# Taking the maximum of attention logits by image column first, and adding the column bias to 32 maxima

## The chip, the cores and the metric

The kernel runs on one NeuronCore of a Trainium2 chip, in float32 throughout. The metric is the device time of one execution in microseconds (us); lower is better. A second, profiled execution gives the trace. The engines are named as in the profile: PE (TensorE's matmuls), PEld (its weight loads), DVE (VectorE), ACT (ScalarE), POOL (GpSimd) and SP (the queue that issues the DMAs).

## The reference

Eight images of 32 x 32 pixels with 256 channels go through two layers: a hybrid of convolution and attention, and then attention with a mixture of experts. The change is in the attention of the first layer, which has 8 heads of 8 channels and a logit with three terms:

```
logits  = einsum('bnid,bnjd->bnij', q, k)     # i: query pixel, j: key pixel, 1024 each
logits += rel_w                               # depends on the query and on the key's column
logits += rel_h                               # depends on the query and on the key's row
weights = softmax(logits, axis=-1)
attn    = einsum('bnij,bnjd->bnid', weights, v)
```

The softmax needs the maximum of each query's logits over 1024 keys. In the kernel's names a key is a pair (x, y): x is the image row, y the column (0 to 31 each). So a logit is s(x, y) + w(y), where s holds the product and the row term and w is the column term.

## The kernel before, in words

Images are handled one after the other in a loop over `b`. For each, `conv_layer_inputs` normalizes the image, computes keys, queries and values, and builds the relative terms: `rh` holds the row terms, `rwq` (128 queries x 8 tiles x 2 head groups x 128) the column terms with queries on partitions, as `(y h)` with h one of four heads. `conv_layer_attention` does the attention and, beside it, the 3 x 3 convolution (L398, its results added by VectorE in L406). `attention_layer` does the second layer's attention; the experts come at the end, for all images.

Inside `conv_layer_attention` the work is cut into four `Unit`s of an image: two groups of four heads (`HG = 4`) times two halves of the queries. A unit loads its tile `F` by DMAs on SP's queue (L423, L427, L434: row terms, queries, column terms), and then passes through three sweeps:

- `score` (16 per unit, two per step): for 128 queries and one head, two products (L448) of 24 rows of `F` with 512 columns of `km` each fill `lg`, a PSUM tile of 2 x 512. There are two such tiles. VectorE then reads the tile in L457: it adds the column term, spread over the 32 image rows, and keeps the maximum, which goes to one column of `mx`. A second instruction of L457 reads out the accumulated maximum.
- `fold` (L465 to L474, once per unit): the 16 columns of maxima are negated, transposed, added to the row terms and written into `F` by DMA, so that the next sweep gets logits less their maximum.
- `weigh` (32 per unit, four per step): the product (L483) for 128 keys and 512 queries into a PSUM tile `st` (three of them), and ScalarE's exponential (L490) from there to `PT`. `gather` (L498) multiplies `PT` of a finished key tile with the values, four products per step that use all 128 rows of the array. At the end of a unit come `close` and `settle` (L508 to L518).

A product of 24 or 32 rows occupies one of four groups of 32 rows of the array; products on different groups run side by side. `r = 32 * ((hl + 2 * a) % HG)` says which group.

PE's order is written out by hand in a loop over steps `s` (`tc.manual_schedule`). Step `s` issues `score(2j)`, `weigh(k, 1)`, `weigh(k, 3)`, `score(2j + 1)`, `weigh(k, 0)`, `gather` of the step before, `weigh(k, 2)`. Weighing starts 10 steps after scoring (`lead = NT + LAG`). In these first 10 steps there is nothing to weigh, and the image's 144 convolution products are spread over them (`if not weigh and left`). Steps 10 to 31 score and weigh; steps 32 to 41 only weigh. The order of the other engines is set by the framework from the program's order and the tiles' dependences.

`km` holds the keys' side of both products, in the order `p e (x y)`: 4 blocks `e` of 8 columns, and in each 16 image rows x by 8 columns y. `weigh` takes a block of 128 as it lies. `score` reads it through a view, `p x e y`, so that the 512 columns of `lg` come in the order of image rows, each with its 32 columns.

Of the kernel before, what the change touches and what calls it, by code (L numbers as in the profile page):

```python
# [9 lines left out]
FP = mybir.dt.float32  # L10
I32 = mybir.dt.int32
AF = mybir.ActivationFunctionType
ALU = mybir.AluOpType
AX = mybir.AxisListType
PSUM = bass.MemoryType.PSUM

P = 128
B, HH, WW, C = 8, 32, 32, 256
# [4 lines left out]
HG = 4  # L23
# [12 lines left out]
def kernel(  # L36
# [26 lines left out]
    nc = tc.nc  # L63
# [29 lines left out]
    with ExitStack() as ph:  # L93
        wp = ph.enter_context(tc.tile_pool(name="wp", bufs=1))
        work = ph.enter_context(tc.tile_pool(name="work", bufs=1))
# [15 lines left out]
        def lg_tile(name):  # L111
            return ps_lg.tile([P, 2, 512], FP, tag="lg", name=name)
# [80 lines left out]
        KM = []  # L193
# [215 lines left out]
        class Unit:  # L409
# [32 lines left out]
            def score(self, n, rwq):  # L442

                i, hl = divmod(n, HG)
                lg = lg_tile("lg")
                for a in range(2):
                    r = 32 * ((hl + 2 * a) % HG)
                    nc.tensor.matmul(  # L448
                        lg[:, a, :],
                        lhsT=self.F[r : r + 24, a, 0, i * P : (i + 1) * P],  # L450
                        rhs=KM[self.g][r : r + 24, a].rearrange("p e (x y) -> p x e y", y=8),
                        start=True,
                        stop=True,
                    )
                lv = lg.rearrange("p a (x y) -> p (a x) y", y=WW)
                bias = rwq[:, self.half * 4 + i, self.g, hl::HG].unsqueeze(1).to_broadcast([P, HH, WW])
                nc.vector.tensor_tensor_reduce(  # L457
                    lv, lv, bias, 1.0, -3.0e38, op0=ALU.add, op1=ALU.max, accum_out=self.mx[:, i, hl : hl + 1]
                )

            def fold(self, n):

                mc = mcols[n % 2]
                for c in (0, 64):
                    nc.vector.tensor_scalar(mc[:, :, c : c + HG], self.mx, -1.0, None, ALU.mult)  # L465
                pm = st_tile("pmx")
                for i in range(4):
                    nc.tensor.transpose(pm[0:68, i * P : (i + 1) * P], mc[:, i, :], ident)
                mb = work.tile([P, 512], FP, tag="mb", name="mb")
                nc.vector.tensor_tensor(mb[0:68], pm[0:68], self.rh[0:68], ALU.add)  # L470
                F = self.F
                for a, r, c in ((0, slice(0, P, 32), slice(0, 4)), (1, slice(64, P, 32), slice(64, 66)), (1, slice(0, 64, 32), slice(66, 68))):
                    k = c.stop - c.start
                    nc.sync.dma_start(out=F[r, a], in_=mb[c].unsqueeze(1).to_broadcast([k, 4, 512]))  # L474
# [55 lines left out]
        def conv_layer_attention(b, kq, rh, rwd, rwq):  # L530
# [7 lines left out]
            for s in range(NU * NT + lead + 2):  # L538
# [3 lines left out]
                if j == 0 and 0 < u < NU - 1:  # L542
                    units.append(Unit(u + 1, kq, rh, rwd))
                score, weigh = u < NU, 0 <= w < NU
                if score:
                    units[u].score(2 * j, rwq)
# [212 lines left out]
    work = ctx.enter_context(tc.tile_pool(name="fwork", bufs=2))  # L759
# [148 lines left out]
    for b in range(B):  # L908
# [22 lines left out]
        for q in range(2):  # L931
            hT = work.tile([P, TOPK * NF, 512], FP, tag="hT", name="hT")
            for k in range(TOPK):
                for f in range(NF):
                    phd = ps_h.tile([P, 512], FP, tag="h", name="phd")
                    for kc in range(KC):
# [3 lines left out]
                            rhs=n2T[:, kc, q * 512 : (q + 1) * 512],  # L940
# [6 lines left out]
            r = work.tile([P, 4, C], FP, tag="r", name="r")  # L947
            st = work.tile([P, 4, 6], FP, tag="fst", name="fst")
            mv = work.tile([P, 4, 2], FP, tag="fmv", name="fmv")
            for j in range(4):  # L950
                py = ps_y.tile([P, C], FP, tag="y", name="py")
                nc.tensor.matmul(py, lhsT=dbc[:, b, :], rhs=b2sb, start=True, stop=False)  # L952
                for k in range(TOPK):
                    for f in range(NF):
# [3 lines left out]
                            rhs=ws[k][1][:, f, :],  # L958
# [6 lines left out]
            y = work.tile([P, 4, C], FP, tag="yo", name="yo")  # L965
# [58 lines left out]
```

## Time and profile before

| | us |
|---|---|
| median of 3 runs | 3249.84 (3228.76 to 3250.91) |
| profiled execution | 3222.47, its span 3220.7 |
| PE busy | 2910.0 (90% of the span) |
| VectorE busy | 1707.5 (53%) |
| ScalarE busy | 966.6 (30%) |
| GpSimd busy | 291.6 (9%) |
| L448 (scores), 2048 matmuls | 599.7 |
| L457 (maxima), 512 tiles | 1011.7, and 87.8 for reading the accumulator |
| L483 (weigh), 2048 matmuls | 695.6 |
| L490 (exponentials), 1024 | 568.1 |

The span is the time from the first to the last instruction of the profiled execution; the device time lies 1.8 us above it. The profiled execution is 27 us below the median of the three runs. Busy time counts an instruction from its start to its end; the ends of matmuls are modelled, and a busy PE can be waiting within. An fp32 product shows up as two matmul instructions (passes). Rows of groups give the busy time in us, the mean time of one instruction in ns, then the idle time of the engine before them and what ended it. The granted clock of PE (PEclk) is a share of full speed: in this trace it is 1.00 or 0.50, with a mean of 0.911.

### The profile page before, as it was taken

To read this page: it belongs to the slowest core of one execution; us is meant where nothing else is said; L and a number is where in the kernel's file an instruction comes from. 1 tells how busy PE (TensorE), PEld (TensorE's weight loads), DVE (VectorE), ACT (ScalarE), POOL (GpSimd) and SP (SyncE) were. 2 spreads that over 40 slices of the span, in tenths; PEclk is the share of its full clock that TensorE was granted. 3 is DMA by queue.
4 is the path that set the end of the run, shared out by engine and by line. 5 is a ranking of instruction groups with operands and counts; after the bars stand their busy time and mean duration, and the time that the engine had idled before them with its cause. 6 is when DMAs were issued, how large, how long until landed. Compare 5 with 4: busy or idle time off the path is not lost.

```text
span 3220.7 us, 40512 instructions
## 1 busy us (share of the span) xinstructions
PE 2910.0 (90%) x16473; PEld 1691.7 (53%) x16473; DVE 1707.5 (53%) x2734; ACT 966.6 (30%) x1657; POOL 291.6 (9%) x321
## 2 busy tenths in 40 slices
PE   5998899889988998899889998899889986999999
PEld 4633673367335832584257425753565344666665
DVE  4792469245934594448444844486448734233322
ACT  1153105420542054204520352035302531323222
POOL 4001100110011000100011001100110012112110
PEclk7999789979998899889987998799979997999999
DMA  3310131014100510051004100410032102112110
GB/s 101 57 29 1 56 67 29 1 42 81 29 2 29 93 29 2 27 92 32 2 27 93 30 4 14 92 36 12 1 78 37 25 1 95 66 63 81 53 59 20
DMA packets 83753, 135.75 MB, mean 42 GB/s; under 512 B 12000, under 2 KB 40552, under 8 KB 81520
## 3 DMA queue, kind: packets, MB, share of 16 engines
q1 hardware_dynamic: 80976, 131.20, 18.0%
q8 instruction: 130, 2.13, 0.3%
q10 hardware_dynamic: 2592, 1.97, 0.2%
q14 instruction: 55, 0.45, 0.1%
HBM read 53.43 MB, written 25.17 MB: 24 GB/s over the span
## 4 chain that ended last, share of the span: by engine, by line
PE 80%; DVE 8%; issue 6%; ACT 3%; SPq 1%; DMA 1%; POOL 1%; ACTq 0%; DVEq 0%; POOLq 0%
PE pc L398 13%; PE st L483 11%; PE lg L448 10%; PE py L955 7%; PE phd L937 7%; PE po L498 7%; PE lg L593 4%; PE po L705 3%; PE prel L338 3%; PE pq L673 2%; PE tp L610 2%; PE pk L294 2%; PE pmean L736 2%; PE py L952 1%; DVE lg L457 1%
## 5 line engine op out<-in xcount | busy, mean ns | idle before, releaser
L457 DVE CUSTOM_DVE_ANT_1 lg<-lg,rwq 128x1024 f32<-128x1024 f32 x512 | 1011.7, 2041 | 212.5 <-PE lg L448 194.0
L483 PE MATMUL st<-F,km 32*128 32x512 f32 x2048 | 695.6, 655 | 46.1 <-ACT PT L490 45.5
L490 ACT ACTIVATE PT<-st 128x512 f32<-128x512 f32 x1024 | 568.1, 597 | 556.0 <-PE st L483 526.0
L448 PE MATMUL lg<-km,F 24*128 24x512 f32 x2048 | 599.7, 650 | 22.1 <-DVE mx L457 13.6
L398 PEld LDWEIGHTS pc<-convw,gpad 128*128 128x128 f32 x2304 | 388.5, 197 | 66.7 <-issue 66.7
L398 PE MATMUL pc<-convw,gpad 128*128 128x192 f32 x2304 | 412.1, 339 | 0.0
L483 PEld LDWEIGHTS st<-F,km 32*128 32x128 f32 x2048 | 213.2, 186 | 340.8 <-ACT PT L490 306.7
L448 PEld LDWEIGHTS lg<-km,F 24*128 24x128 f32 x2048 | 198.7, 191 | 207.2 <-DVE mx L457 113.7
L498 PE MATMUL po<-PT,v 128*32 128x512 f32 x2048 | 285.7, 619 | 0.0
L955 PE MATMUL py<-w,hT 128*128 128x256 f32 x1024 | 237.3, 385 | 0.0
L937 PE MATMUL phd<-n2T,w 128*128 128x512 f32 x512 | 224.3, 596 | 0.0
L658 POOL TENSOR_TENSOR T<-T,n 128x256 f32<-128x256 f32 x64 | 47.2, 752 | 1933.5 <-DVE n L653 1933.5
L955 PEld LDWEIGHTS py<-w,hT 128*128 128x128 f32 x1024 | 189.9, 190 | 45.6 <-issue 22.4
L962 DVE TENSOR_TENSOR r<-py,n 128x256 f32<-128x256 f32 x64 | 27.2, 425 | 309.3 <-PE py L955 309.3
L517 DVE RECIPROCAL rc<-pa 128x16 f32<-128x16 f32 x32 | 8.9, 277 | 297.8 <-PE pa L514 297.8
L490 ACT ACT_TABLE_LOAD x8 | 10.3, 1283 | 498.2 <-PE st L483 498.2
L937 PEld LDWEIGHTS phd<-n2T,w 128*128 128x128 f32 x512 | 97.2, 191 | 115.3 <-issue 108.2
L498 PEld LDWEIGHTS po<-PT,v 128*32 128x32 f32 x2048 | 41.7, 109 | 205.0 <-issue 199.4
L593 PE MATMUL lg<-k,q 128*128 128x512 f32 x256 | 129.1, 624 | 0.0
L705 PE MATMUL po<-pt,v 128*128 128x256 f32 x512 | 120.5, 381 | 5.5 <-DVE pt L613 5.5
L596 DVE TENSOR_REDUCE nm<-lg 128x1 f32<-128x1024 f32 x64 | 78.4, 1224 | 80.2 <-PE lg L593 80.2
L944 ACT ACTIVATE hT<-phd,b1c 128x512 f32<-128x512 f32 x128 | 86.3, 686 | 97.0 <-PE phd L937 96.8
(212 smaller groups left out, 2664.5 us busy)
## 6 DMA issues: line engine op xcount, KB each, us to landing
F<-rh SPq DMA_DIRECT2D x256, 128.0 KB
F<-kq SPq DMA_DIRECT2D x256, 64.0 KB
F<-rwd SPq DMA_DIRECT2D x256, 64.0 KB
w<-in_L_ffn_W_dram SPq DMA_DIRECT2D x32, 512.0 KB
T<-in_x_dram SPq DMA_DIRECT2D x8, 1024.0 KB
rwd<-rw SPq DMA_DIRECT2D x16, 512.0 KB
Td<-T SPq DMA_DIRECT2D x8, 1024.0 KB
T<-Td SPq DMA_DIRECT2D x8, 1024.0 KB
```

Source lines behind the costliest of these rows:

```text
L338: nc.tensor.matmul(dst, lhsT=lhsT, rhs=kqv[rows, :, a], start=True, stop=True)
L398: nc.tensor.matmul(pc[:, 0:CO], lhsT=gflat[:, dx, kc, t * P + dy * WW : (t + 1) * P + dy * WW], rhs=convw[:, i, :], start=i == 0, stop=i = ...
L448: nc.tensor.matmul(lg[:, a, :], lhsT=self.F[r : r + 24, a, 0, i * P : (i + 1) * P], rhs=KM[self.g][r : r + 24, a].rearrange("p e (x y) -> ...
L457: nc.vector.tensor_tensor_reduce(lv, lv, bias, 1.0, -3.0e38, op0=ALU.add, op1=ALU.max, accum_out=self.mx[:, i, hl : hl + 1])
L483: nc.tensor.matmul(st, lhsT=KM[self.g][r : r + 32, a, e, :], rhs=self.F[r : r + 32, a, e, :], start=True, stop=True,)
L490: nc.scalar.activation(self.pts[j][:, hl, :], st, AF.Exp)
L498: nc.tensor.matmul(self.po[32 * hl : 32 * hl + 32, :], lhsT=v32[:, j, self.g * HG + hl, :], rhs=pt[:, hl, :], start=j == 0, stop=j == NT - 1,)
L593: nc.tensor.matmul(lg[:, h, :], lhsT=q, rhs=k[:, h * 512 : (h + 1) * 512], start=True, stop=True)
L705: nc.tensor.matmul(po[:, 0:IB], lhsT=v1[:, jc, :], rhs=pt[:, jc, :], start=jc == 0, stop=jc == NT - 1)
L937: nc.tensor.matmul(phd, lhsT=ws[k][0][:, kc, f * P : (f + 1) * P], rhs=n2T[:, kc, q * 512 : (q + 1) * 512], start=kc == 0, stop=kc == KC - 1,)
L944: nc.scalar.activation(hT[:, k * NF + f, :], phd, AF.Gelu, bias=b1c[:, f, k * B + b : k * B + b + 1])
L955: nc.tensor.matmul(py, lhsT=hT[:, k * NF + f, j * P : (j + 1) * P], rhs=ws[k][1][:, f, :], start=False, stop=k == TOPK - 1 and f == NF - 1,)
```

## The change

The logits' maximum is taken in two stages. The maximum over the image rows x comes first, for each column y: a plain reduce of `lg` into 32 numbers, which leaves the column term out, since it is the same for all rows. The 32 numbers of four heads are collected in a new tile `my` (32 columns by 4 heads). After the fourth head the column term is added to all 128 numbers, and a second reduce takes the maximum over the columns for the four heads at once. The products of `score` read `km` through another view, `p e y x` in place of `p x e y`: the 512 columns of `lg` now come by image column, each with its 16 rows, and in `km` one column of the moving operand lies 8 elements (32 bytes) from the one before it. Instruction for instruction, the order of PE stays as it was. The diff shifts later lines by 7.

```diff
             def score(self, n, rwq):
 
                 i, hl = divmod(n, HG)
+                if hl == 0:
+                    self.my = work.tile([P, WW, HG], FP, tag="my", name="my", bufs=2)
+                my = self.my
                 lg = lg_tile("lg")
                 for a in range(2):
                     r = 32 * ((hl + 2 * a) % HG)
                     nc.tensor.matmul(
                         lg[:, a, :],
                         lhsT=self.F[r : r + 24, a, 0, i * P : (i + 1) * P],
-                        rhs=KM[self.g][r : r + 24, a].rearrange("p e (x y) -> p x e y", y=8),
+                        rhs=KM[self.g][r : r + 24, a].rearrange("p e (x y) -> p e y x", y=8),
                         start=True,
                         stop=True,
                     )
-                lv = lg.rearrange("p a (x y) -> p (a x) y", y=WW)
-                bias = rwq[:, self.half * 4 + i, self.g, hl::HG].unsqueeze(1).to_broadcast([P, HH, WW])
-                nc.vector.tensor_tensor_reduce(
-                    lv, lv, bias, 1.0, -3.0e38, op0=ALU.add, op1=ALU.max, accum_out=self.mx[:, i, hl : hl + 1]
-                )
+
+                nc.vector.tensor_reduce(
+                    my[:, :, hl], lg.rearrange("p a (y x) -> p y a x", y=WW), AX.XY, ALU.max
+                )
+                if hl == HG - 1:
+                    nc.vector.tensor_tensor(
+                        my, my, rwq[:, self.half * 4 + i, self.g].rearrange("p (y h) -> p y h", h=HG), ALU.add
+                    )
+                    nc.vector.tensor_reduce(self.mx[:, i, :], my.rearrange("p y h -> p h y"), AX.X, ALU.max)
```

## The prediction

> **What bounds the kernel now.** I read the costliest groups first, then looked at one image (82 to 274 us of the trace) stage by stage, and last at what each engine waits for in the stage in which the change works.
>
> The groups of the page, with some of the longer list that keeps shapes apart:
>
> ```profile
> L457 DVE CUSTOM_DVE_ANT_1 lg<-lg,rwq 128x1024 f32<-128x1024 f32 x512 | 1011.7, 2041 | 212.5 <-PE lg L448 194.0
> L483 PE MATMUL st<-F,km 32*128 32x512 f32 x2048 | 695.6, 655 | 46.1 <-ACT PT L490 45.5
> L490 ACT ACTIVATE PT<-st 128x512 f32<-128x512 f32 x1024 | 568.1, 597 | 556.0 <-PE st L483 526.0
> L448 PE MATMUL lg<-km,F 24*128 24x512 f32 x2048 | 599.7, 650 | 22.1 <-DVE mx L457 13.6
> ...
> L457 DVE DVE_READ_ACCUMULATOR2_ANT mx<- 128x1 f32 x512 | 87.8, 171 | 0.0
> ...
> L596 DVE TENSOR_REDUCE nm<-lg 128x1 f32<-128x1024 f32 x64 | 78.4, 1224 | 80.2 <-PE lg L593 80.2
> ...
> L350 DVE COPY rw<-prel 128x512 f32<-128x512 f32 x32 | 30.2, 1022 | 76.9 <-PE prel L338 76.9
> ```
>
> L457 is the largest group of VectorE: 2.04 us for each of 512 tiles. L596 takes the maximum of a PSUM tile of the same size in 1.22 us, so a plain maximum costs 0.82 us less. L448 has 2048 matmul instructions for 1024 products: an fp32 product runs as two passes.
>
> Next the stages of the first image, cut where the first and the last `weigh` and the last `score` start:
>
> ```profile
> core 0: us, PE busy (x) PEld busy (x) DVE busy (x) ACT busy (x) POOL busy (x), PEclk, DMA share, GB/s
> 82.00:138.00 56.00, 56.00 (x350) 47.13 (x349) 38.32 (x46) 0.00 (x0) 0.00 (x0) 1.00 0.43 79
> 138.00:232.00 94.00, 91.04 (x526) 31.79 (x528) 87.50 (x96) 48.87 (x88) 0.00 (x0) 0.96 0.14 25
> 232.00:274.00 42.00, 37.29 (x184) 10.12 (x178) 4.82 (x9) 23.30 (x43) 0.00 (x0) 1.00 0.01 2
> ```
>
> Three stages, alike in all eight images. **Lead** (10 steps, scores and convolution): PE never idles, VectorE has a third of the time free. **Mixed** (22 steps, scores, exponentials and gathers): VectorE is busy 87.5 of 94 us. **Tail** (no scores): PE and ACT alone. So VectorE can set the pace in the mixed stage only. The waits of its steady part, 150 to 232 us, say that it does, mildly:
>
> ```profile
> PEld st L483 <- ACT PT L490: 16.5, 20, 0.8
> ...
> PEld lg L448 <- DVE mx L457: 13.8, 16, 1.5
> ...
> DVE lg L457 <- PE lg L448: 3.7, 4, 3.1
> ```
>
> VectorE waits 3.7 us for scores, PE waits 13.8 us for VectorE to free a score tile. What stands just behind VectorE is seen in the tail, one step of which is:
>
> ```profile
> 260.81 1.06 PE L498 MATMUL po<-PT,v 128*32 128x512 f32 x8
> ...
> 261.80 1.13 PE L483 MATMUL st<-F,km 32*128 32x512 f32 x6
> 262.96 1.57 ACT L490 ACTIVATE PT<-st 128x512 f32<-128x512 f32 x3 [1.45 <-PE st L483]
> ...
> 263.61 1.12 PE L483 MATMUL st<-F,km 32*128 32x512 f32 x2 [0.67 <-ACT PT L490]
> 264.66 1.06 PE L498 MATMUL po<-PT,v 128*32 128x512 f32 x8
> ```
>
> Gather to gather 3.85 us with no score and no L457: three `st` tiles filled, one exponential, the fourth matmul, the gather. That loop of PE and ACT stays whatever VectorE does. In the mixed stage the gathers of the trace follow each other by 4.11 us (mean of 14 regular steps of each image) and by 4.76 us in the four steps with a `fold` or a `settle`, which cost 4.50 in the tail.
>
> **The change, part by part.**
>
> *VectorE.* Removed: 512 times 2.04 + 0.17 us (L457 and its read of the accumulator, which partly overlaps the next L457). Added: 512 reduces of 128x1024 to 32 columns. By L596 they cost 1.22 us; their reading hops between the two halves of `lg` every 16 columns, which no row shows, so the bounds are 1.22 and L457's own 2.04. I take 1.23, since L596 is the same operation on the same memory and L382, which writes in runs of 8, costs no more than the plain copy L367 (0.69 us for 512 columns both). Added too, per four scores: an add of 128x128 (nearest L518, 0.29 us) and a reduce to 4 columns (nearest L154 below, 0.36 us). Per step of two scores VectorE falls from 4.1 us to 2 x 1.23 + 0.65 / 2 = 2.8 us. The add waits for the fourth reduce and the last reduce for the add, all on VectorE; queued behind them are the next L459 reduce, the convolution's L406, and `fold`'s operations. These come earlier than now, since the queue in front of them is shorter.
>
> In lead and tail none of this is on the path: in the lead L457 and L406 fill 38 of 56 us under a PE that never idles. In the mixed stage the step can fall to the loop: 14 x (4.11 - 3.85) + 4 x (4.76 - 4.50) = 4.6 us per image, 37 for eight; 40 with the two first steps. That is the most the change can bring.
>
> *PE.* No instruction is added or moved: L448 keeps its 2048 passes and `lg` is still written in one run. But the order in which the passes read `km` changes: now runs of 8 columns that lie together, after the change each column is 8 columns (32 bytes) from the one before. Now L448 behaves like a contiguous read: its passes on one row group start 0.43 us apart in the trace, as L593's do. What does a read with a step cost? The trace has one such moving operand, L338 (step of 32 columns), and two strided VectorE operations:
>
> ```profile
> L154 DVE TENSOR_REDUCE esel<-ident x1: 362/362/362, 2.2 to 2.2; 128x32 f32<-128x128 f32 x1
> ...
> L146 DVE TENSOR_REDUCE gsel<-ident x1: 287/287/287, 1.9 to 1.9; 128x16 f32<-128x128 f32 x1
> ...
> 389.36 1.02 DVE L350 COPY rw<-prel 128x512 f32<-128x512 f32 x1 [4.94 <-PE prel L338]
> ```
>
> VectorE pays: L154 reads 128 columns at a step of 128 bytes and takes 75 ns longer than L146, 0.59 ns a column; L350 writes 512 columns at that step in 1022 ns where L367 takes 692, 0.64 ns a column. Contiguous columns cost it (1224 - 692) / 512 = 1.04 ns, so a strided one is about 1.63 to 1.69 ns. PE at half clock (granted 0.50 there) does not pay: from the start of the last weight load of L338 to VectorE's L350 the trace has 505 ns; for L375, same weight load, 64 contiguous columns, to L382 it has 561. The 56 ns between them are 32 columns at 1.67 ns (at half clock the trace has 1095 ns from the last pass of L448, 512 columns, to VectorE and 459 from L923's, 128 columns: 1.66 ns a column). Were strided columns twice as dear, the two would be equal. So memory gives PE a strided column in at most 1.67 ns, and that is all the row says: at full clock PE wants one in 0.43 us / 512 = 0.83 ns. The bounds at full clock are thus 0.43 us a pass (nothing lost) and 512 x 1.67 = 0.85 us. Between them I take 1.64 ns, 0.84 us a pass, by the VectorE rows, which give nearly the time that PE had at half clock: it looks like one limit of the memory, not of an engine.
>
> [...] The row at half clock shows no penalty, the two VectorE rows do. [...]
>
> What 0.41 us a pass cost: in the lead, four products of a step run at once on four row groups, two passes each, and the convolution needs all rows, so the step grows by 2 x 0.41 = 0.83 us. About 9 of the 10 steps run at full clock (the first falls into the half clock of 407 to 413 us in the second image, likewise in the others): 9 x 0.83 x 8 = 59 us, all on PE's path. In the mixed stage the scores run beside `weigh` on other row groups, but one product of each pair shares a row group with the weigh that comes first: 0.96 + 2 x 0.84 + 0.20 us drain = 2.84 us into the step; two reduces end it at 4.07 and 5.30. The next step's first score, due at 3.85, waits for the tile until 4.07, its second one until 5.30 and ends 0.25 us after the gather could start. So the step is 3.85 + 0.25 = 4.10: as now, and the gain is gone. Bounds there: -2 us an image where the waits hide better (-16), and, with a reduce of 1.5 us (a third of the way to its upper bound), ends 0.27 and 0.54 us later, 0.41 a step on the mean, 20 x 0.41 x 8 = 65.
>
> Sum: 0 + 59 + 0, say 60. The profiled execution took 3222.5 us, the median is 3249.8, with runs from 3228.8 to 3250.9; the profile lies 27 us under the median, and I add the 60 to the median: **3310 us**, 1.8% slower. Its own range: 44 us of lead (0.83 + 0.59 = 1.43 ns a column, were VectorE's extra time what counts: 9 x 2 x 0.30 x 8) with -16 in the mixed stage, to 62 with 65, 3278 to 3376.
>
> **The rivals.**
>
> *A: PE reads the step for nothing.* The half-clock row is for it; against it are the VectorE rows. Then only VectorE's relief counts: -24 (a second `score` that still holds the row group of a weigh for 0.1 us a step) to -40, about -36: 3214 us.
>
> *B: the strided reduce is the dear part.* PSUM hops make L459 as dear as L457 was (2.04 us), PE pays nothing. VectorE then needs 4.08 + 0.33 = 4.41 us a step against 4.11: 20 x 0.30 x 8 = 48 us slower, 3298. It decides from a reduce of 1.9 us on. Against it: L596, and that the runs of 16 are longer than those of L382, which cost nothing.
>
> **How the numbers follow.** Forecast 0.67, A 0.25, B 0.08. A measurement of this kernel tells about 1% from no change. A lies on that border: 0.14 of it is faster by over 1%, 0.11 within. The forecast gives 0.05 within 1%, 0.62 slower, B 0.01 and 0.07. Together 0.14, 0.17, 0.69. The range reaches from most of A to the upper end of the forecast: 3206 to 3370.
>
> **What would show it.** Right: L448's successor with passes 0.8 us apart on a row group, the lead stage longer by 7 us an image (62.7 to 67.0 us from first score to first weigh now), the mixed stage about 93.6 us as now, VectorE busy some 390 us less, L459 near 1.23 us. Wrong: passes still 0.43 us apart, the lead unchanged, and mixed-stage gathers 3.85 us apart (A); L459 at 1.9 us or more with VectorE full in the mixed stage (B).

## The result

The changed kernel took 3355.97 us (median of 3 runs, 3351.31 to 3364.85) against 3249.84 us: a ratio of 1.035, with an interval of 1.030 to 1.041. The profiled execution took 3364.85 us, 142 us more than the profiled one before. Single runs of one kernel differ by the clock that PE was granted (in one series of the kernel before, mean clocks of 0.895 to 0.915 went with 3271 to 3217 us), so sums are made stage by stage below.

The groups of the profile page after; L451, L459, L490, L497 and L505 were L448, L457, L483, L490 and L498:

```profile
L459 DVE TENSOR_REDUCE my<-lg 128x32 f32<-128x1024 f32 x512 | 604.1, 1221 | 619.4 <-PE lg L451 599.7
L451 PE MATMUL lg<-km,F 24*128 24x512 f32 x2048 | 746.7, 1108 | 0.4 <-issue 0.4
L497 ACT ACTIVATE PT<-st 128x512 f32<-128x512 f32 x1024 | 558.1, 598 | 641.5 <-PE st L490 330.5
L490 PE MATMUL st<-F,km 32*128 32x512 f32 x2048 | 697.8, 657 | 41.0 <-ACT PT L497 40.5
```

VectorE's reduce costs 1.22 us, as L596 did, and now waits 600 us for scores. The scores' passes went from 650 to 1108 ns while `weigh`, which reads the same `km` as it lies, stayed at 657. One burst of eight score passes in the lead stage, from the timeline of PE, before and then after:

```profile
108.87 1.14 PE L448 MATMUL lg<-km,F 24*128 24x512 f32 x8
```

```profile
105.61 2.09 PE L451 MATMUL lg<-km,F 24*128 24x512 f32 x8
```

Four row groups run two passes each, side by side: the four first passes start within 0.02 us of each other. A burst is longer by 0.95 us. In the trace the second pass of a burst now starts 0.98 us after the first (0.53 before, 0.11 of which is the first weight load), and two passes in the middle of a row of strided ones start 0.90 us apart (0.43 before).

The stages of the first image, cut as before at the first and last `weigh` and the last `score`, with the columns as there:

```profile
82.00:146.70 64.70, 64.70 (x353) 47.03 (x351) 27.65 (x38) 0.00 (x0) 0.00 (x0) 1.00 0.37 69
146.70:244.00 97.30, 97.30 (x524) 35.31 (x525) 59.39 (x73) 47.02 (x86) 0.00 (x0) 1.00 0.14 24
244.00:286.40 42.40, 38.37 (x187) 10.88 (x180) 4.52 (x9) 23.88 (x44) 0.00 (x0) 1.00 0.01 2
```

In the mixed stage VectorE has fallen from 87.5 us to 59.4, and the stage is longer all the same: PE fills all of it. Over the eight images, from the first score to the first weigh the trace has 591.5 us (524.8 before), from there to the last score 812.9 (748.7). So the lead lost 67 us and the mixed stage 64; the rest of the 142 lies mostly in the tails (8.5).

The waits from 160 to 244 us:

```profile
DVE my L459 <- PE lg L451: 29.0, 18, 2.6
ACT PT L497 <- PE lg L451: 26.4, 18, 2.1
PEld st L490 <- ACT PT L497: 21.4, 28, 0.8
...
PEld lg L451 <- DVE my L459: 2.6, 10, 0.4
```

VectorE now waits for scores, and so does ScalarE (26.4 us; 4.3 us in 150 to 232 us of the trace before): its exponentials wait for a matmul that they don't read.

### The profile page after: what moved, and what is told of

Same layout as the page of the kernel before. It is cut to its first block, busy times and chain, and to the rows that moved or that the text cites. A ratio compares the mean times of both kernels' runs of the same rounds, so it can differ in the third digit from the quotient of the medians.

```text
span 3363.1 us, 39832 instructions
## 1 busy us (share of the span) xinstructions
PE 3080.3 (92%) x16473; PEld 1731.4 (51%) x16473; DVE 1380.8 (41%) x2478; ACT 956.3 (28%) x1657; POOL 291.1 (9%) x321
## 4 chain that ended last, share of the span: by engine, by line
PE 90%; DVE 6%; ACT 2%; issue 1%; POOL 1%; DMA 0%; SPq 0%; ACTq 0%; DVEq 0%; POOLq 0%
PE lg L451 15%; PE st L490 15%; PE pc L398 12%; PE po L505 8%; PE py L962 7%; PE phd L944 7%; PE po L712 3%; PE lg L600 3%; PE prel L338 3%; PE pq L680 2%; PE prel L341 2%; PE tp L617 2%; PE pk L294 2%; PE pmean L743 2%; PE py L959 1%; PE pvv L375 1%
## 5 line engine op out<-in xcount | busy, mean ns | idle before, releaser
L459 DVE TENSOR_REDUCE my<-lg 128x32 f32<-128x1024 f32 x512 | 604.1, 1221 | 619.4 <-PE lg L451 599.7
L451 PE MATMUL lg<-km,F 24*128 24x512 f32 x2048 | 746.7, 1108 | 0.4 <-issue 0.4
L497 ACT ACTIVATE PT<-st 128x512 f32<-128x512 f32 x1024 | 558.1, 598 | 641.5 <-PE st L490 330.5
L490 PE MATMUL st<-F,km 32*128 32x512 f32 x2048 | 697.8, 657 | 41.0 <-ACT PT L497 40.5
L490 PEld LDWEIGHTS st<-F,km 32*128 32x128 f32 x2048 | 229.9, 191 | 451.2 <-ACT PT L497 354.9
L505 PE MATMUL po<-PT,v 128*32 128x512 f32 x2048 | 292.4, 633 | 0.0
L451 PEld LDWEIGHTS lg<-km,F 24*128 24x128 f32 x2048 | 190.3, 192 | 105.7 <-issue 52.3
L505 PEld LDWEIGHTS po<-PT,v 128*32 128x32 f32 x2048 | 42.1, 110 | 228.5 <-issue 223.7
L712 PEld LDWEIGHTS po<-pt,v 128*128 128x128 f32 x512 | 94.7, 190 | 29.3 <-DVE pt L620 7.5
```

The lines of the kernel that those rows point to most:

```text
L451: nc.tensor.matmul(lg[:, a, :], lhsT=self.F[r : r + 24, a, 0, i * P : (i + 1) * P], rhs=KM[self.g][r : r + 24, a].rearrange("p e (x y) -> ...
L459: nc.vector.tensor_reduce(my[:, :, hl], lg.rearrange("p a (y x) -> p y a x", y=WW), AX.XY, ALU.max)
L490: nc.tensor.matmul(st, lhsT=KM[self.g][r : r + 32, a, e, :], rhs=self.F[r : r + 32, a, e, :], start=True, stop=True,)
L497: nc.scalar.activation(self.pts[j][:, hl, :], st, AF.Exp)
L505: nc.tensor.matmul(self.po[32 * hl : 32 * hl + 32, :], lhsT=v32[:, j, self.g * HG + hl, :], rhs=pt[:, hl, :], start=j == 0, stop=j == NT - 1,)
L712: nc.tensor.matmul(po[:, 0:IB], lhsT=v1[:, jc, :], rhs=pt[:, jc, :], start=jc == 0, stop=jc == NT - 1)
```

## The experiments

**The change without its read on PE.** `km` is read as before, and VectorE takes the step instead:

```diff
-rhs=KM[self.g][r : r + 24, a].rearrange("p e (x y) -> p e y x", y=8),
+rhs=KM[self.g][r : r + 24, a].rearrange("p e (x y) -> p x e y", y=8),
...
-my[:, :, hl], lg.rearrange("p a (y x) -> p y a x", y=WW), AX.XY, ALU.max
+my[:, :, hl], lg.rearrange("p a (x y) -> p y a x", y=WW), AX.XY, ALU.max
```

> Two-stage maximum as in the change, but PE reads km as before (runs of 8 columns) and VectorE's reduce reads lg at a step of 32 columns instead. Theory (the strided moving read on PE is the whole loss): passes of the scores 0.43 us apart, lead stage back to 62.7 to 67.0 us; if the reduce stays near 1.22 us the mixed stage falls to gathers 3.85 us apart and the time to about 37 us below the kernel before (ratio 0.989). Rival 1 (the two-stage maximum on VectorE is the loss: its chain of reduce, add, reduce): the time stays near the changed kernel, ratio about 1.03. A reduce made dear by the step in PSUM would show as a mean of 1.6 us or more and a ratio between 0.99 and 1.02.

Measured: ratio 0.9904 (0.9869 to 0.9938), 3209.9 us beside 3244.6. Lead 527.4 us; regular gathers 3.85 us apart. The groups:

```profile
L459 DVE TENSOR_REDUCE my<-lg 128x32 f32<-128x1024 f32 x512 | 605.0, 1221 | 443.8 <-PE lg L451 402.2 <-PE st L490 41.5
...
L451 PE MATMUL lg<-km,F 24*128 24x512 f32 x2048 | 519.8, 642 | 9.2 <-DMA F<-rwd 3.8 <-DMA F<-kq 3.4 <-issue 2.0
```

The two-stage maximum is the gain that was worked out for it, and rival 1 falls. VectorE reads PSUM at a step of 32 columns in the same 1.22 us. This version beats both kernels, the kernel before by 1%.

**The read on PE without the two-stage maximum.** The kernel before with the new view of `km` alone:

```diff
-rhs=KM[self.g][r : r + 24, a].rearrange("p e (x y) -> p x e y", y=8),
+rhs=KM[self.g][r : r + 24, a].rearrange("p e (x y) -> p e y x", y=8),
```

> The kernel before with one thing of the change, PE's strided read of km; L457 is left as it was, so the column term meets other columns than its own (that part of the result is left out). Theory: passes 0.90 us apart; lead longer by the 8.3 us an image of the changed kernel (67 in all); in the mixed stage the scores end 2.96 us into a step and two maxima of 2.0 us follow, so the step grows from 4.11 to about 4.9 to 5.0 us (130 to 150 us in all): 200 to 220 us above before, ratio 1.06 to 1.07. Rival 1 (the two-stage maximum is the loss): ratio 1.00, since nothing of it is here. Rival 2 (the clock granted to PE falls): passes 0.43 us in the stretches at full clock and 0.85 us elsewhere, with a mean clock well below 0.91.

Measured: ratio 1.0997 (1.0933 to 1.106), 3552 us. The lead lost 68.6 us, as expected; the mixed stage 217, more than the 130 to 150 expected: regular gathers 5.4 us apart on the mean, and 6.5 in steps with `fold` or `settle`, which had not been counted. Part of this is the clock. In the two images whose mixed stage ran at a mean clock of 0.95 (0.96 before) it took 113 us in place of 93.6, which would be 155 us for eight, close to what was expected; in the other six the clock was 0.81 to 0.89 and the stage took 120 to 127 us. No run here tells why the clock was lower there. The changed kernel, with the same read, takes 3356 us: the two-stage maximum is worth far more where the scores are late, though part of the difference is again the clock.

**The order changed at the source**, so that both read runs:

```diff
-kv = km[:, a].rearrange("p g (x y) -> p g x y", y=8)
+kv = km[:, a].rearrange("p g (y x) -> p g x y", y=8)
...
-kq[0:DK, q * 512 : (q + 1) * 512].rearrange("p (e x y) -> p x e y", e=4, y=8),
+kq[0:DK, q * 512 : (q + 1) * 512].rearrange("p (e y x) -> p x e y", e=4, y=8),
...
-xn[:, kc, a * 4 + e].rearrange("p (x y) -> p x y", y=8),
+xn[:, kc, a * 4 + e].rearrange("p (y x) -> p x y", y=8),
...
-rhs=KM[self.g][r : r + 24, a].rearrange("p e (x y) -> p e y x", y=8),
+rhs=KM[self.g][r : r + 24, a].rearrange("p e k -> p (e k)"),
```

> The change with km laid out by image column at its source (the one-hot rows, the keys written by L303 and the copies of L280 take the order y, x within a block), so that score reads 512 columns that lie together and VectorE does just what it does in the changed kernel. Theory: passes 0.43 us apart, lead 62.7 to 67.0 us, regular gathers of the mixed stage 3.85 us apart: 37 us below the kernel before, less about 5 us for the strided writes of L303 at the start of each image, ratio 0.99. Rival 1 (the two-stage maximum is the loss): about the changed kernel's time, ratio 1.03. Rival 2 (clock): no clear change against the changed kernel beyond its clock.

Measured: ratio 0.9994 (0.9954 to 1.0033). Rival 1 falls here too: L459 stays at 1.22 us, passes are 0.43 us apart, the mixed stage has 720.7 us, to the tenth what the first experiment has. But the 32 us that were expected did not show in the median. The runs had lower mean clocks (0.877 to 0.904, where the first experiment's had 0.888 to 0.910); at 0.904 both took 3212 to 3213 us, and the kernel before 3245 to 3250. Whether the lower clock comes with this version or was chance is not settled. L303 rose from 0.74 to 1.08 us by its strided write.

**The reading order by image.** Each image reads `km` in another order:

```diff
+def step(s, t=1):
+    return lambda k: k.rearrange("p (c s t) -> p s c t", s=s, t=t) if t > 1 else k.rearrange("p (c s) -> p s c", s=s)
+KEYS = [lambda k: k, step(2), step(4), step(8), step(16), step(4, 2), step(8, 2), step(4, 4)]
...
+rhs=KEYS[b](KM[self.g][r : r + 24, a].rearrange("p e k -> p (e k)")),
```

> The changed kernel with another reading order of km in each of the eight images (for seven of them the columns of lg are out of order, so the column term is added to other columns): step of 1, 2, 4, 8 and 16 columns, then runs of 2 columns at a distance of 8, runs of 2 at a distance of 16, runs of 4 at a distance of 16. [...] Rival (the cost grows with the distance): step 2 above 0.43, step 16 above step 8. Rival 2 (any interrupted run costs): runs of 2 well above 0.43. At half clock all of them are 0.85 to 0.90 us if it is a limit of the memory's side, and double the full-clock values if it is PE's.

Measured in the lead bursts at full clock, nine in each image, all within 1 ns; from the first pass of a row group to its second, which is one pass and 0.11 us of weight load:

| order of the 512 columns | us |
|---|---|
| step 1 | 0.533 |
| step 2 (8 bytes) | 0.556 |
| step 4 (16 bytes) | 0.966 |
| step 8 (32 bytes) | 0.982 |
| step 16 (64 bytes) | 0.929 |
| runs of 2, 8 columns apart | 0.564 |
| runs of 2, 16 columns apart | 0.539 |
| runs of 4, 16 columns apart | 0.533 |

In these rows the cliff lies between steps of 8 and 16 bytes (0.556 and 0.966 us), distance beyond it does not add (0.982 at 32 bytes, 0.929 at 64), and two columns that lie together are enough to avoid it (0.539 and 0.564). Its price is 0.45 us on 512 fp32 columns (0.982 less 0.533), 0.88 ns each. At half clock (granted 0.50) the same burst has 1.015 us for runs of 8 (the kernel before) and 1.087 to 1.092 for step 8: 0.07 us in place of 0.45. So the strided column takes about 1.7 to 1.8 ns at either clock (0.90 us / 512 at full clock; at half clock an estimate, 1.66 ns for a contiguous column and 0.07 us / 512 more), and at half clock PE, which takes those 1.66 ns for a contiguous one, hardly wants it sooner.

**Half of the reduce**, to see whether the late scores of the mixed stage wait for VectorE:

```diff
-my[:, :, hl], lg.rearrange("p a (y x) -> p y a x", y=WW), AX.XY, ALU.max
+my[:, :, hl], lg[:, 0].rearrange("p (y x) -> p y x", y=WW), AX.X, ALU.max
```

> The changed kernel with L459 reading only the first half of each lg tile (half of the keys are left out of the maximum), so that VectorE needs about 0.69 us a score (L367's time for 512 columns) where it needed 1.22; PE's strided read stays. It splits the loss of the mixed stage. Theory (in regular steps the late scores meet VectorE's two reduces and the two lg tiles; in the steps with fold or settle PE alone is late): lead as in the changed kernel (71.3 to 75.3 us); regular gathers 3.9 us throughout in place of 3.91 and 4.64 to 4.74 in turn, save that after every fourth score the add and the second reduce may still delay one; the steps with fold or settle stay at 5.69. Mixed stage 5 us an image shorter. Rival (PE alone is late in the regular steps as well): they stay at 4.35 on the mean.

```profile
L459 DVE TENSOR_REDUCE my<-lg x512: 680/693/696, 76.0 to 2721.5; 128x32 f32<-128x512 f32 x171
```

The reduce fell to 0.69 us and nothing moved: regular gathers of 3.91, 4.64 and 4.74 us and those of 5.69 stand where they stood. The theory for the regular steps fell with it. (This kernel and the others that ran only once are read by their steps: 3405 us here, 3377 with one product strided, 3420 with both alterations, 3329 with the row groups apart.) The trace showed the wait of the exponentials instead:

```profile
198.41 0.60 ACT L497 ACTIVATE PT<-st 128x512 f32<-128x512 f32 x1 [1.41 <-PE st L490]
200.31 1.08 ACT L497 ACTIVATE PT<-st 128x512 f32<-128x512 f32 x2 [1.30 <-PE lg L451]
```

The product that the exponential at 200.31 reads was done at 198.40 us in the trace; a score issued ahead of it ended at 200.24.

**One of the two products strided:**

```diff
-rhs=KM[self.g][r : r + 24, a].rearrange("p e (x y) -> p e y x", y=8),
+rhs=KM[self.g][r : r + 24, a].rearrange("p e (x y) -> p e y x" if a == 0 else "p e (x y) -> p e x y", y=8),
```

> The changed kernel with only the first product of each score (a = 0) reading km at the step of 8 columns; the second reads runs of 8 as before (its columns of lg are then out of order, and the column term is added to other columns). Theory (each row group of the array waits for its own read, and the slowest of the four sets the end): the lead loses as much as with both, 66 us in all against the kernel before, with half of the strided passes; strided passes still 0.90 us, the others 0.43. Rival (one memory limit shared by the row groups): strided passes nearer 0.65 us and the lead loses about half, 33 us. In the mixed stage the strided product of every second score stands on a row group with a weigh ahead of it, so its loss is most of the 64 us: 40 to 60.

Measured: the lead lost 65 us with half of the strided passes, as with all of them (67); in a burst the strided passes start 0.98 us apart and the others 0.54. So here the row groups do not share the limit, and the slowest of four sets the end. The mixed stage lost 67 us, above the range expected, but two of its images were at half clock for long (115 and 114 us). The other six had 94 to 100 us, 25 in all above the kernel before, which would be 33 for eight: below the range.

**The weighs ahead of the score**, after a new theory: the exponentials of weigh 1 and 3 wait for the strided score that PE was given ahead of them (exponentials waited 26.4 us for scores from 160 to 244 us of the changed kernel's trace).

```diff
-if score:
-    units[u].score(2 * j, rwq)
 if weigh:
     units[w].weigh(k, 1)
     units[w].weigh(k, 3)
+if score:
+    units[u].score(2 * j, rwq)
 if score:
     units[u].score(2 * j + 1, rwq)
```

> The changed kernel with PE's order altered within a step: weigh 1 and weigh 3 are issued ahead of the first score, not behind it. The strided read stays. New theory (in the mixed stage the exponentials of weigh 1 and 3 wait for PE's one counter, which also counts the strided score issued ahead of them; so their st tiles come free late, the next step's weighs start late, and the score behind them in the same row group ends after the gather could start): with the weighs ahead, the exponentials of a step follow each other without a gap, regular gathers 3.9 to 3.95 us in place of 4.35 on the mean, 14 x 0.42 x 8 = 47 us less than the changed kernel; the steps with fold or settle stay at 5.69, where the last score is late by itself; lead unchanged. Time about 1.4% below the changed kernel, ratio to before near 1.02. Rival (the row groups alone: the score behind a weigh is late whatever ACT does): regular gathers stay at 4.35 and the time near the changed kernel's.

Measured: ratio 1.0417 (1.0308 to 1.0525), no gain where 47 us were expected. The exponentials now follow each other without the gap, but the gathers of 4.64 only became 4.51 to 4.59, and those of 4.74 stayed. In a step of 4.51 (gathers at 168.63 and 173.15 us) the late score starts at 171.14 us, just when VectorE's reduce (169.87 plus 1.22 us) has freed its tile: the wait that the half reduce had taken away.

**The same alteration without the strided read** (on the first experiment's kernel):

> The kernel that reads km in runs of 8 on PE and lg at a step on VectorE, with the same alteration of PE's order. Its regular gathers are 3.85 us apart already, which is the loop of three st tiles, and its steps with fold or settle 4.72: no change expected from either theory, ratio 0.99. If the counter holds it up as well, steps with fold or settle would fall towards 4.50, 7 us in all.

Measured: ratio 0.9979 (0.9936 to 1.0022); its mixed stage has 703.3 us, regular gathers 3.855, `fold` and `settle` 4.76. As expected the order brings nothing there; the median lies higher than the first experiment's with a lower clock (0.886 to 0.908), and at 0.905 both took 3207 to 3212 us.

**Both alterations at once**, half reduce and weighs first:

> Both alterations at once on the changed kernel: L459 reads only the first half of lg (half of the keys are left out of the maximum; 0.69 us on VectorE), and weigh 1 and 3 are issued ahead of the first score. The strided read stays. Theory (a late score is held by two things of nearly equal length, the wait for VectorE to free its lg tile and the wait of the exponentials for PE's counter, so that taking away either shows nothing): with both gone the regular gathers are 3.9 us apart throughout, the mixed stage of an undisturbed image some 5 us shorter than the 97.3 us of the changed kernel's shortest; steps with fold or settle stay at 5.6 to 5.8, lead unchanged at 71 to 76 us. Rival (the row groups alone hold up every second score): regular gathers alternate between 3.9 and 4.6 to 4.75 as before.

Measured: the gathers of 4.64 are gone (3.9), those of 4.74 remain, each fourth one, and the shortest mixed stage has 95.0 us, 2 less where 5 were expected. So two waits of nearly equal length did hold the former, and something else holds the latter. One late step in the timeline of PE:

```profile
198.29 0.70 PE L490 MATMUL st<-F,km 32*128 32x512 f32 x3
198.31 1.16 PE L451 MATMUL lg<-km,F 24*128 24x512 f32 x1
198.82 0.60 PE L490 MATMUL st<-F,km 32*128 32x512 f32 x3
199.25 2.01 PE L451 MATMUL lg<-km,F 24*128 24x512 f32 x7
201.07 1.03 PE L490 MATMUL st<-F,km 32*128 32x512 f32 x2
202.03 0.64 PE L505 MATMUL po<-PT,v 128*32 128x512 f32 x4
```

The third weigh starts at 201.07, 2.78 us into the step, when the last strided passes (200.16, 0.90 us) end. Every four key tiles `a` changes, and the third weigh falls on the row group in which the last weigh and a score already stand.

**The row groups kept apart**, on top of that kernel:

```diff
-units[w].weigh(k, 0)
+units[w].weigh(k, 0 if k < 4 else 2)
...
-units[w].weigh(k, 2)
+units[w].weigh(k, 2 if k < 4 else 0)
```

> The kernel with half the reduce and the weighs first, with one alteration more: for the second four key tiles of a unit, heads 0 and 2 change places in the order of weighing, so that the last weigh of a step is always on row group 2 and the third of the next step always on row group 0. (Half of the keys are left out of the maximum, as there.) In that kernel every fourth regular gather was still 4.74 us after the one before, and in the trace the third weigh of such a step starts just when the second strided pass of a score ends. Theory (where the third weigh falls on the row group of the last weigh before it, it stands behind that weigh and two strided passes, 0.96 + 2 x 0.90 = 2.76 us into the step, not 1.9): with the row groups apart the gathers of 4.74 become 3.9, all regular ones are 3.9; steps with fold or settle stay at 5.7. Rival (something else recurs every four steps, such as the add and the second reduce on VectorE): 4.74 stays.

```profile
197.32 0.70 PE L490 MATMUL st<-F,km 32*128 32x512 f32 x3
...
199.24 1.03 PE L490 MATMUL st<-F,km 32*128 32x512 f32 x2
200.22 1.06 PE L505 MATMUL po<-PT,v 128*32 128x512 f32 x8
201.22 0.70 PE L490 MATMUL st<-F,km 32*128 32x512 f32 x3
...
203.14 1.03 PE L490 MATMUL st<-F,km 32*128 32x512 f32 x2
204.12 0.64 PE L505 MATMUL po<-PT,v 128*32 128x512 f32 x4
```

At full clock all regular gathers are 3.9 us apart, the third weigh 1.92 us into each step. The mixed stage has 91.0 to 91.5 us in six of eight images (97.3 at the least in the changed kernel), with the strided read still there; steps with `fold` or `settle` stay at 5.69 to 5.9. The swap was run only on top of the other two alterations, not on the changed kernel alone.

## Why the prediction was right or wrong

**Right.** The read of `km` at a step of 32 bytes is the whole loss: with it alone the kernel before is 10% slower (part of it by a lower clock), without it the change is 1% faster. A limit per column that does not follow PE's clock, and that the half-clock row could not show it, hold: at half clock the price is 0.07 us a pass, at full clock 0.45. The value taken from VectorE's strided rows, 1.64 ns, was near the measured 0.90 us / 512 = 1.76; that both come from one limit of the memory was an analogy, which no run here shows. The upper bound of 0.85 us a pass was too low: the row's 56 ns over 32 columns are 1.75 ns, not 1.67, and with them the bound is the 0.90 us that was measured. The lead term was 59 us; measured 67, since 9 bursts x 8 images x 2 x 0.45 is 65. VectorE's relief was sized right: 37 us forecast where PE pays nothing; at equal clock (0.904) the first experiment is 32 to 37 us under the kernel before. L459 came in at 1.22 us, so rival B falls; rival A is the first experiment's kernel, not the changed one.

**Wrong: the mixed stage**, entered with 0 and measured at 64 us. That term failed in three ways. First, the steps with `fold` or `settle` had no term of their own, and there the scores set the end. They start behind the transposes, 2.6 us after the gather, and the next gather follows their last passes. A step with `settle`, before and then after:

```profile
183.20 0.66 PE L514 MATMUL pa<-ident,os 128*128 128x128 f32 x4
183.78 0.70 PE L448 MATMUL lg<-km,F 24*128 24x512 f32 x2
...
185.87 1.07 PE L498 MATMUL po<-PT,v 128*32 128x512 f32 x8
```

```profile
191.59 0.66 PE L521 MATMUL pa<-ident,os 128*128 128x128 f32 x4
192.17 1.16 PE L451 MATMUL lg<-km,F 24*128 24x512 f32 x2
...
194.21 1.09 PE L451 MATMUL lg<-km,F 24*128 24x512 f32 x1
...
195.23 1.07 PE L505 MATMUL po<-PT,v 128*32 128x512 f32 x8
```

From the first score to the gather it was 2.09 us and is 3.06, so these steps take 5.69 us in place of 4.76, which is 0.93 x 4 x 8 = 30 us. Without the strided read (first experiment) these steps take 4.71 us, with half of it 5.5. That the scores set the end is read from the trace; no run changed these steps alone. Second, regular steps were costed at 4.10 by VectorE's two reduces. The runs show five in each image at 4.74, by the shared row group, and two or three at 4.64, by two waits of which either alone holds the step up; VectorE by itself explains none. The 14 regular steps add up to 5 x 4.74 + 2 x 4.64 + 7 x 3.91 = 60.4 us against 57.5, 23 us in all. Third, some 12 us are left, in the first steps of the stage, where the stretches at half clock differ from image to image (107.8 us in the second image, 27 of them at half clock; 97.3 in the first, none of them; 7 in each image before); no run here tells what sets those stretches.

The prediction also said of VectorE's busy time 390 us less; it is 327 on the page, since the accumulator's reads (87.8 us in all) had overlapped the next L457: in the trace before, one of each starts at 190.85 us.

The forecast of 3310 us was 46 short; on the profiled executions the sum of 60 was short by 82, of which the mixed stage is 64. That the median missed by less is luck: the profiled execution lay 27 us under the median before the change and 9 us above it after. It is luck too that the stated range holds the time: its upper end allowed 65 us in the mixed stage for a reduce of 1.5 us, and the reduce took 1.22; the 64 us came from elsewhere.

## What to carry to other kernels

A moving operand of TensorE is best read in runs of at least two fp32 columns (0.53 to 0.56 us from a burst's first pass to its second here, a step of two included; 0.93 to 0.98 at wider steps); where a transposed view is needed, let VectorE take the step in PSUM, where here it cost nothing (a reduce of 1.22 us with the step and without). A row taken at half clock can hide a limit in absolute time (a price of 0.07 us a pass here, 0.45 at full clock): ask what the same row would have to do at full clock. And where an engine is late by two waits of like length, removing either can show next to nothing (gathers of 4.64 us stayed, or fell to 4.51 to 4.59; with both waits removed they were 3.9); remove both before a theory is dropped.

## What the runs showed of the hardware

A strided fp32 column cost PE about 1.7 to 1.8 ns at both clocks (0.90 us / 512 at full clock; at half clock an estimate, the prediction's 1.66 ns for a contiguous column and 0.07 us / 512 more), step 16 a little less than step 8 (0.929 and 0.982 us from a burst's first pass to its second). VectorE's maximum over PSUM took 1225 ns (the median) for 1024 columns with a step of 32 columns, in runs of 16, or straight on. ScalarE's exponentials also waited for scores that PE had been given ahead of their own matmul: with half of the reduce, one whose matmul was done at 198.4 us started at 200.3, when a score issued ahead of it ended; with the weighs issued first the gap was gone. Matmuls on different row groups overtook each other, as that one (198.4 us) had overtaken the score (200.24), but on one row group they queued: with both alterations, the third weigh of a step started at 201.07 us, when the strided passes ahead of it on its row group ended (200.16 plus 0.90).
